# A selective-scan kernel: smaller weight preparation and earlier loads in the head, and one more step between six products and their uses

## The chip, the cores and the metric

The kernel runs on one core of one Trainium2 chip. The time is device time in microseconds (us) from the first to the last instruction. The core has five engines that work at the same time: TensorE (PE, matrix products, with its weight loads PEld shown apart), VectorE (DVE), ScalarE (ACT), GpSimd (POOL) and SyncE (SP), which here only issues DMAs. The kernel before takes 5404.86 us (median of 3 runs, 5400.69 to 5408.01).

## The reference, cut to what matters

The input x is 4 images of 64 x 64 positions with 96 channels. A block of projections with the signs of inputs and weights, a 3 x 3 convolution and a selective scan in four directions is followed by an attention and a feed-forward layer (those last two are in the kernel as "sums", "middle" and "last").

```python
xz = bilinear(x, W_in, s_in, b_in)            # sign(x) @ (s * sign(W - mean)).T + b
xp, z = jnp.split(xz, 2, axis=-1)
t = conv3x3(sign(xc + move0), sc * sign(conv_W)) + conv_b + rp_b0
t = jnp.where(t >= 0, t, prelu_a * t) + rp_b1 + xc
xconv = silu(t)                               # u of the scans, 192 channels
# four orders of the 4096 positions: rows, columns, and both reversed
dts_r, Bs, Cs = split(bilinear(xin, Wl, sl, bl))
delta = softplus(bilinear(dts_r, Wd, sd, bd) + dt_bias)
A = -jnp.exp(A_logs)                          # 192 channels x 16 states, per order

def step(h, inp):                             # 4096 steps per order and image
    ut, dt, Bt, Ct = inp
    h = jnp.exp(dt[..., None] * A[None]) * h + (dt * ut)[..., None] * Bt[:, :, None, :]
    return h, jnp.einsum('bkdn,bkn->bkd', h, Ct)
# ... y of the four orders is added, normed, gated by z; then W_out, residual, attention, feed-forward
```

## The kernel before

The scans are cut into pieces: 4 images x 4 orders (KORD is 1, 3, 0, 2) x 4 stretches of 1024 positions x 6 groups of 32 channels x 4 groups of 4 states, 1536 pieces in all, each a tile of 128 x 1024. Per piece there is a decay dA (ScalarE), an injection (delta u times B), a scan (VectorE), a product with C (on VectorE or GpSimd, whichever has less to do by a running account) and a reduction (TensorE).

```python
def decay(self, i):                    # ScalarE, into one of 2 PSUM tiles
    t = c.p.dA.tile([128, CH], F32, name=f"dA_{i}", tag="dA")
    c.nc.scalar.activation(t, self.dlt[i // NQ][0], AF.Exp, scale=c.anm[:, g, ...])

def inject(self, i):                   # GpSimd
    t = c.p.w.tile([128, CH], F32, name=f"w_{i}", tag="w")
    c.gps.tensor_tensor(t, self.dlt[i // NQ][1], self.bt[b, e, ci, q], ALU.mult)

def run(self, back):                   # Scans
    for _ in self.start(): pass
    self.decay(0)
    for i in range(AHEAD): self.inject(i)          # AHEAD is 3
    for i in range(n):
        self.loads(i)
        if i % NQ == 1:
            while KORD[self.pieces[i][1]] == 2 and self.pieces[i][0] not in c.turned:
                next(back)             # order 2 needs the turned y of orders 1 and 3
            self.load_sums(i)
        ... # carry, decay(i + 1), evacuate, reduce(i - 4), inject(i + AHEAD), product, scan(i)
        next(back, None)               # one step of the background work per piece
```

The background work is a generator that ends a step at each yield: the preparation (prologue) of a later image, the turn of y, and the epilogue of an earlier image.

```python
def back():
    yield from first                   # rest of the prologue of image 0
    yield from prologue(c, 1)
    for b in range(NB):
        while not scans.done(b, 2): yield
        if b not in c.turned: yield from turn(c, b)
        if b + 2 < NB: yield from prologue(c, b + 2)
        e = ends[b]; e.open()
        yield from e.sums(e.lane)      # 8 chunks of 512 positions: norms, W_out, attention sums
        if b + 1 < NB:
            if scans.done(b + 1, 2, 20):
                while not scans.done(b + 1, 2): yield
                yield from turn(c, b + 1)
            yield from e.middle()
            yield from e.last(e.lane)  # 8 chunks: attention output and feed-forward

def turn(c, b):                        # columns to rows, 16 tiles; two halves share one buffer
    ts = [load(*part) for part in parts[:5]]
    yield; yield
    for n, (h, q) in enumerate(parts):
        if q == 0:
            yh = tn.tile([96, L], F32, name=f"yh{h}_{b}", tag="yh")
            for _ in range(4 * h): yield
        yield
        nc.scalar.copy(yh[...], ts.pop(0)[...])
        if n + 5 < len(parts): ts.append(load(*parts[n + 5]))
        if q == NQ8 - 1: nc.sync.dma_start(c.y13[b][h], yh)

# one chunk of the epilogue's norm, cut: each product is used one step later
mm(ps, [(c.mean[:, 0], ys[h]), (c.mean[:, 1], ys[1 - h])])   # yc
yield
nc.scalar.activation(t, sq[h], AF.Square)
mm(ps, [(c.on192, sq[0]), (c.on192, sq[1])])                 # var
yield
nc.scalar.activation(sd, var, AF.Ln, bias=eps)
# ... xc -> xq, xv -> xr, kv -> kvs in the same way; in last(): fv -> fr
```

The head runs before the scans. Two generators take turns: weights() makes the small constants, and the prologue of image 0 ("alone", with the engines to itself) makes the inputs of the scans.

```python
def weights():
    wrow = temp("wrow", [96, 2, 96], F32)          # ln_w broadcast to 96 rows, by DMA
    for rows, h, s in halves(a["pv"][:, :, LN_W]):
        nc.sync.dma_start(wrow[:, h, rows], s.partition_broadcast(96))
    # ... signs of W_in, of the convolution weights, of Wl ...
    # Wd: signs put into zeroed tiles by 8 + 32 copies, 64 transposes, 8 evacuations
    for s in range(8):
        nc.gpsimd.tensor_copy(e[:, :, s, NR * s : NR * s + NR], wds[0])
    for k in range(NK):
        transposed(wdz[0:48, k]..., [e[:, k, s, :] for s in range(8)])
    # ... the same for wdy ...
    for g in range(NG):                            # A, 4 bytes at a time
        src = a["al"][...].rearrange("d k (q j) -> j d (k q)", j=4)
        for j in range(4):
            nc.sync.dma_start(anm[j::4, g, :], src[j])

# prologue of image 0, cut
for q in range(NQ8):                               # x transposed, 8 x 512 columns
    ...; xfin(q, ps)                               # sign by ScalarE, x + b_out by VectorE
nc.gpsimd.memset(xgw[64:128, 1], 0.0)              # clear the padded inputs
for h in range(2): nc.gpsimd.memset(tflat[h].bitcast(F32), 0.0)
# project(h, q): ix, iz products, then signs tp and sz
# convolution in 16 parts: v, r, cz, sign sg (to xg by DMA), e, u; u stored to ud and, turned, to utd
# rows: xg turned (xr), Wl products (acc); B and C (tbc) to bcd, signs (sgn) to sgd, in two halves gh
for x, k in enumerate((o, o + 2)):
    nc.sync.dma_start(gw[:, x, 16:64], c.sgd[b][k]...)
    if fast and x: c.loads_ahead()                 # loads of B and u for the first scans

# Scans.start(), cut
self.next_part = self.prepare(); next(self.next_part)
lanes = [part(0), part(1)]                         # the first deltas, from gT and wdz
while lanes: interleave(lanes)
nc.scalar.activation(c.anm, c.anm, AF.Exp)
nc.vector.tensor_scalar(c.anm, c.anm, -1.0, None, ALU.mult)
for n in range(3):
    ... # two broadcasts of delta and delta u (dl_s), 512 KB each
    if n == 0:
        for q in range(NQ): self.load_bc(1, self.ct, 0, 0, 0, q)     # C
```

Of the kernel before, what the change touches and what calls it, by code (L numbers as in the profile page):

```python
# [53 lines left out]
def hybrid_kernel(ctx: ExitStack, tc: tile.TileContext, a: dict, out: bass.AP):  # L54
# [108 lines left out]
    def weights():  # L163
# [73 lines left out]
        wrow = temp("wrow", [96, 2, 96], F32)  # L237
        for rows, h, s in halves(a["pv"][:, :, LN_W]):
            nc.sync.dma_start(wrow[:, h, rows], s.partition_broadcast(96))
        for rows, h, s in halves(a["pv"][:, :, LN_B]):  # L240
            nc.sync.dma_start(meanw[96:97, 0, h, rows], s.unsqueeze(0))
# [19 lines left out]
        for t in gTs + [wdz]:  # L261
            nc.gpsimd.memset(t.bitcast(F32), 0.0)
# [16 lines left out]
        def scales():  # L279
            part = temp("part", [96, 2, 2])  # L280
            for i in range(2):
                for h in range(2):
                    nc.vector.tensor_reduce(part[:, h, i : i + 1], cwn[h][i], AX.X, ALU.add, apply_absolute_value=True)
            nc.vector.tensor_tensor(csc, part[:, :, 0], part[:, :, 1], ALU.add)
            nc.vector.tensor_scalar(csc, csc, 1.0 / (9 * DN), None, ALU.mult)

            nc.vector.tensor_tensor(cbias, pv[:, :, CONV_B], pv[:, :, RP0], ALU.add)
            nc.vector.tensor_tensor(acs, pv[:, :, PRELU], csc, ALU.mult)
            nc.vector.tensor_tensor(acb, pv[:, :, PRELU], cbias, ALU.mult)
            nc.vector.tensor_tensor(acb, acb, pv[:, :, B_X], ALU.add)  # L290
            nc.vector.tensor_tensor(acb, acb, pv[:, :, RP1], ALU.add)
            nc.vector.tensor_scalar(oma, pv[:, :, PRELU], -1.0, 1.0, ALU.mult, ALU.add)
            for h in range(2):
                nc.gpsimd.tensor_scalar(omad[:, h], i96, oma[:, h : h + 1], None, ALU.mult)
# [5 lines left out]
        for o in range(2):  # L300
# [16 lines left out]
            yield  # L317
            transposed(wR[:, o].rearrange("p x m -> p (x m)"), [we[:, x, :] for x in range(4)])
            yield
            if o == 0:  # L320
                scales()
                yield


        wds = []
        for x, t in enumerate(wd):
            wdm = negmean(f"wdm{x}", t, NR)
            wds.append(temp(f"wds{x}", [128, NK, NR], BF16))
            for k in range(NK):
                nc.scalar.activation(wds[x][:, k, :], t[:, k, :], AF.Sign, bias=wdm[:, k : k + 1])  # L330
        e = temp("wde", [128, NK, 8, 48], BF16)
        nc.gpsimd.memset(e, 0.0)
        for s in range(8):
            nc.gpsimd.tensor_copy(e[:, :, s, NR * s : NR * s + NR], wds[0])
        yield
        for k in range(NK):
            transposed(wdz[0:48, k].rearrange("p s d -> p (s d)"), [e[:, k, s, :] for s in range(8)])
            yield
        for k2 in range(0, NK, 2):
            e = temp(f"wdf{k2}", [128, 2, 8, 128], BF16)  # L340
            nc.gpsimd.memset(e, 0.0)
            for r0 in (0, 64):
                for s in range(8):
                    at = r0 + NR * s
                    nc.gpsimd.tensor_copy(e[r0 : r0 + 64, :, s, at : at + NR], wds[1][r0 : r0 + 64, k2 : k2 + 2])
            yield
            for k in range(2):
                transposed(wdy[:, k2 + k].rearrange("p s d -> p (s d)"), [e[:, k, s, :] for s in range(8)])
                yield
# [11 lines left out]
        nc.vector.memset(mean[:, 1], -1.0 / DN)  # L361
        for h in range(2):
            for o in range(2):
                nc.vector.tensor_tensor(meanw[0:96, h, o], mean[:, int(h != o)], wrow[:, o], ALU.mult)
# [24 lines left out]
        for k in range(NK):  # L389
            o, r0 = k % 2, 64 * (k // 2)  # L390
            nc.sync.dma_start(sbR[r0 : r0 + 32, o, 0:1], a["sl_bc"][0:32, k : k + 1])
            nc.sync.dma_start(sbR[r0 : r0 + 32, o, 1:2], a["bl_bc"][:, 32 * k : 32 * k + 32].rearrange("o p -> p o"))
            nc.sync.dma_start(sbR[r0 + 32 : r0 + 32 + NR, o, :], a["sl_dt"][k])
        for g in range(NG):
            src = a["al"][32 * (g % 4) : 32 * (g % 4) + 32, g // 4].rearrange("d k (q j) -> j d (k q)", j=4)
            for j in range(4):
                nc.sync.dma_start(anm[j::4, g, :], src[j])
# [66 lines left out]
def run(c):  # L464

    scans = Scans(c)
    c.loads_ahead = scans.first_loads
# [63 lines left out]
def prologue(c, b, xts=None):  # L531
# [11 lines left out]
    with tc.tile_pool(name=f"xg_{b}", bufs=1) as xgp:  # L543
# [3 lines left out]
        with tc.tile_pool(name=f"cv_{b}", bufs=1) as cvp:  # L547
# [5 lines left out]


# [35 lines left out]
            def xfin(q, ps):  # L590
                cols = slice(512 * q, 512 * q + 512)
                nc.scalar.activation(xsT[:, cols], ps, AF.Sign, bias=negm, saturate=False)
                t = f32(f"xb{q}")[0:96]
                if alone:
                    nc.vector.tensor_scalar(t, ps, c.bo, None, ALU.add)
                else:
                    nc.scalar.activation(t, ps, AF.Identity, bias=c.bo)
                c.later.store(c.xbd[b][:, cols], t)

            for q in range(NQ8):  # L600
                ps = bank(f"xps{q}", q % 2)[0:96]
                for i in range(4):
                    nc.tensor.transpose(ps[:, 128 * i : 128 * i + 128], xts[q // 2][:, 4 * (q % 2) + i, :], ident)
                yield
                xfin(q, ps)
# [4 lines left out]
            nc.gpsimd.memset(xgw[64:128, 1], 0.0)  # L610
            for h in range(2):
                nc.gpsimd.memset(tflat[h].bitcast(F32), 0.0)
# [99 lines left out]
            def alone_parts():  # L712

                mid = end = None
                for n, part in enumerate(parts + [None, None]):
# [4 lines left out]
                    for s in range(4):  # L720
# [25 lines left out]
                        elif s == 3 and end:  # L746
                            eh, eq, epz, e, en = end
                            u = f32("u" + en)[0:96]
                            c.vec.tensor_tensor(u, epz, e, ALU.mult)
                            c.later.store(c.ud[b][eh][:, 512 * eq : 512 * eq + 512], u)  # L750
# [78 lines left out]
        with tc.tile_pool(name=f"rw_{b}", bufs=1) as rw:  # L829
            xrs = rw.tile([128, 96, 64], BF16, name=f"xr_{b}", tag="xr")  # L830

            tbc = rw.tile([128, L // 2], F32, name=f"tbc_{b}", tag="tbc")
            sgw = rw.tile([128, L // 8], F32, name=f"sgn_{b}", tag="sgn")
            sgn = sgw.bitcast(F8)
            tbg, sgg = (t.rearrange("p (g r) -> p g r", r=64) for t in (tbc, sgn))
# [8 lines left out]
            for o in (1, 0):  # L844
# [30 lines left out]
                for gh in range(2):  # L875
                    groups = slice(32 * gh, 32 * gh + 32)
                    prev = None
                    for n in range(5):
                        if prev is not None:
# [3 lines left out]
                            if fast:  # L883
                                nc.vector.tensor_scalar(tbg[:, :, dv], sv, sc[0], sc[1], ALU.mult, ALU.add)
                            else:
                                nc.scalar.activation(tbg[:, :, dv], sv, AF.Identity, scale=sc[0], bias=sc[1])
# [27 lines left out]
                    for kk in range(2):  # L914
                        k, r0 = o + 2 * kk, 64 * kk
                        nc.sync.dma_start(c.bcd[b][k][:, L // 2 * gh : L // 2 * gh + L // 2], tbc[r0 : r0 + 32, :])
# [3 lines left out]
                        )  # L920
                    yield
# [66 lines left out]
class Epilogue:  # L988
# [143 lines left out]

    def norm(self, ln, q, got):
# [28 lines left out]
        yield  # L1162
        for h in range(2):
# [8 lines left out]
        yield  # L1172
        sd, var, eps = (f32("sd"), ps[0:96], c.eps5[0:96]) if alone else (y0[96:97], ps[96:97], c.eps5[96:97])
# [45 lines left out]
        yield  # L1219
        t = f32("xq")  # L1220
# [3 lines left out]
        yield  # L1224
        r = self.rstd(ln, f"xr{q}", ps)
# [564 lines left out]
```

## Time and profile before

| | value |
|---|---|
| time, median of 3 | 5404.86 us |
| span of the profiled execution | 5405.6 us, 62146 instructions |
| VectorE busy | 5013.4 us (93%) |
| GpSimd busy | 4962.1 us (92%) |
| ScalarE busy | 3617.6 us (67%) |
| TensorE busy | 3405.6 us (63%) |
| GpSimd product, 128 x 1024 | 2359 ns |
| VectorE product, 128 x 1024 | 1225 ns |
| VectorE scan, 128 x 1024 | about 2.3 us |

In a timeline line the columns are start, duration, engine, line, operation, tiles, count, and in brackets the idle time before with what ended it. "SPq" is SyncE's sequencer issuing a DMA[...]. A line of the waits gives the waiting engine with tile and line, the releaser, then total us, times and the longest. Line 435 is a helper that issues VectorE's and GpSimd's operations, so these are told apart by their tiles.

### The profile page before, as it was taken

The page shows a single profiled execution, that of the slowest core. Times are in us where ns is not written, and L with a number is a line of the kernel's source. Part 1 is how long each engine was busy: PE and PEld are TensorE (multiplying, and loading weights), DVE is VectorE, ACT ScalarE, POOL GpSimd, SP SyncE. Part 2 cuts the span into 40 slices and gives each one's busy share as a digit, 9 for nine tenths or more (in the row PEclk, how much of TensorE's full clock was granted, in tenths as well). Part 3 has the DMA queues.
Part 4 walks back from the last instruction along what each step waited for, and adds up shares of the span by engine and source line. Part 5 has one row for each costly group of instructions (what it writes and reads, how often), then busy time and mean ns, then how long its engine had stood idle before and what let it go on. Part 6 is the DMA issues. An engine that isn't in the chain of part 4 may idle for free. (4 is left out here: it accounts for less than half of the span.)

```text
span 5405.6 us, 62146 instructions
## 1 busy us (share of the span) xinstructions
PE 3405.6 (63%) x20083; PEld 1351.6 (25%) x20083; DVE 5013.4 (93%) x3171; ACT 3617.6 (67%) x5648; POOL 4962.1 (92%) x2293
## 2 busy tenths in 40 slices
PE   6456765467755776656775477566776664444577
PEld 3222222122222322222222233122332221111223
DVE  4599999999999999998999999999999999999995
ACT  5567776677766667777777666677656775565554
POOL 3599999999999999999999999999999999999990
PEclk7667876678866787767887688667787666666788
DMA  4665666777766656666765666766665665666652
GB/s 76 158 216 192 192 207 206 227 225 220 218 180 192 220 189 204 217 219 214 225 205 185 199 218 193 245 211 200 207 214 179 192 201 199 189 224 196 214 176 64
DMA packets 635740, 1068.80 MB, mean 198 GB/s; under 512 B 249723, under 2 KB 366740, under 8 KB 633620
## 3 DMA queue, kind: packets, MB, share of 16 engines
q1 hardware_dynamic: 633028, 1063.89, 63.7%
q8 instruction: 157, 2.57, 0.2%
q14 instruction: 171, 1.40, 0.1%
q0 software_dynamic: 1536, 0.79, 0.1%
q10 hardware_dynamic: 848, 0.15, 0.0%
HBM read 829.75 MB, written 228.30 MB: 196 GB/s over the span
## 5 line engine op out<-in xcount | busy, mean ns | idle before, releaser
L435 POOL TENSOR_TENSOR w<-dl,bc 128x1024 f32<-128x1024 f32 x1524 | 3552.0, 2359 | 52.8 <-PE yp L1578 34.8
L1505 ACT ACTIVATE dA<-dl,anm 128x1024 f32<-128x1024 f32 x1524 | 1701.3, 1116 | 490.5 <-DVE w L435 302.2
L435 DVE TENSOR_TENSOR_SCAN dA<-dA,cy,w 128x1024 f32<-128x1024 f32 x725 | 1698.5, 2343 | 75.0 <-ACT dA L1505 60.8
L435 POOL TENSOR_TENSOR w<-h,bc 128x1024 f32<-128x1024 f32 x570 | 1342.9, 2356 | 118.0 <-DVE h L435 111.0
L1578 PE MATMUL yp<-w,sum 128*32 128x256 f32 x12288 | 1249.9, 503 | 294.0 <-ACT pd L1459 204.7
L435 DVE TENSOR_TENSOR w<-dA,bc 128x1024 f32<-128x1024 f32 x966 | 1183.2, 1225 | 69.9 <-DMA bc<-bcd 8.1
L435 DVE TENSOR_TENSOR_SCAN h<-dA,cy,w 128x1024 f32<-128x1024 f32 x427 | 999.1, 2340 | 9.6 <-ACT dA L1505 9.3
L1578 PEld LDWEIGHTS yp<-w,sum 128*32 128x32 f32 x12288 | 316.3, 127 | 1340.5 <-issue 728.3
L1547 ACT COPY cy<-dA 128x1 f32<-128x1 f32 x725 | 114.0, 157 | 757.0 <-DVE w L435 754.7
L435 DVE TENSOR_TENSOR_SCAN dA<-dA,w 128x1024 f32<-128x1024 f32 x241 | 550.0, 2282 | 26.7 <-ACT dA L1505 25.3
L1440 PE MATMUL dps<-gT,wdz 128*128 128x64 fp8e5 x1008 | 113.0, 310 | 375.6 <-ACT ys L1592 373.5
L435 DVE TENSOR_TENSOR_SCAN h<-dA,w 128x1024 f32<-128x1024 f32 x143 | 325.9, 2279 | 24.6 <-POOL w L435 20.5
L1453 PE MATMUL dps<-sp,ident 128*128 128x512 f32 x378 | 269.5, 801 | 101.5 <-ACT dps L1449 101.5
L1583 PE MATMUL yp<-ya,back 128*128 128x256 f32 x576 | 223.4, 506 | 0.0
L1440 PEld LDWEIGHTS <-wdz 128*128 128x128 fp8e5 x1008 | 92.9, 150 | 449.8 <-issue 448.0
L1440 PE MATMUL dps<-gT,wdy 128*128 128x64 fp8e5 x504 | 57.6, 314 | 213.0 <-ACT ys L1592 212.9
L780 PE MATMUL cv<-tp,cwA 128*96 128x512 fp8e5 x432 | 155.2, 478 | 39.1 <-ACT r L812 38.3
L1105 PE MATMUL yc<-eys,mean 96*96 96x512 f32 x240 | 140.1, 738 | 45.6 <-DVE vks L435 23.9
L1547 ACT COPY cy<-h 128x1 f32<-128x1 f32 x427 | 79.2, 186 | 133.5 <-DVE h L435 132.8
L1445 ACT ACTIVATE pd<-dps,dbias,pvd 128x512 f32<-128x512 f32 x189 | 144.0, 762 | 9.8 <-PE dps L1440 9.5
L1583 PEld LDWEIGHTS yp<-ya,back 128*128 128x128 f32 x576 | 116.8, 234 | 119.0 <-issue 90.4
L1446 ACT ACTIVATE sp<-dps,dbias,pvd 128x512 f32<-128x512 f32 x189 | 144.9, 767 | 0.0
(376 smaller groups left out, 4523.6 us busy)
## 6 DMA issues: line engine op xcount, KB each, us to landing
dl<-dld SPq DMA_DIRECT2D x762, 512.0 KB
bc<-bcd SPq DMA_DIRECT2D x512, 512.0 KB
dld<-pd SPq DMA_DIRECT2D x126, 512.0 KB
yd<-ys SPq DMA_DIRECT2D x764, 64.0 KB
dld<-pd SPq DMA_DIRECT2D x126, 256.0 KB
ya<-yd SPq DMA_DIRECT2D x192, 128.0 KB
pu<-ud SPq DMA_DIRECT2D x32, 512.0 KB
pu<-utd SPq DMA_DIRECT2D x31, 512.0 KB
```

What stands on the lines that cost most here:

```text
L435: return getattr(self.eng, name)(out, *args, **kw)
L780: nc.tensor.matmul(ps, w[:, 96 * h : 96 * h + 96], tp[:, 8 * q + dy : 8 * q + dy + 8, dx : dx + IW], start=(w is taps[0][1]), stop=(w is t ...
L1105: self.c.nc.tensor.matmul(ps, w, x, start=(i == 0), stop=(i == len(pairs) - 1))
L1440: nc.tensor.matmul(pv[:, s], wd[:, k, s], gT[:, :, c0 : c0 + 16], start=(s == 0), stop=(s == 7))
L1445: nc.scalar.activation(d[:, 0], ps, AF.Abs, scale=sc, bias=bi)
L1446: nc.scalar.activation(t, ps, AF.Relu, scale=sc, bias=bi)
L1453: nc.tensor.matmul(ps, c.ident, t, start=False, stop=True, skip_group_check=True)
L1505: c.nc.scalar.activation(t, self.dlt[i // NQ][0], AF.Exp, scale=c.anm[:, g, NQ * KORD[e] + q : NQ * KORD[e] + q + 1])
L1547: self.c.nc.scalar.copy(self.carries[g, q], h[:, CH - 1 : CH])
L1578: c.nc.tensor.matmul(y[32 * x : 32 * x + 32, g % 2, :], c.sum4, prod[:, 256 * x : 256 * x + 256], start=(q == 0), stop=(q == NQ - 1 and no ...
L1583: c.nc.tensor.matmul(y[:, g % 2, :], w, src, start=False, stop=(n == len(more) - 1))
```

## The change

The head: the memsets of the padded inputs come first; x is transposed in four pieces of 1024 columns; ln_w and ln_b are broadcast by one product instead of DMAs of single elements; Wd is transposed in two small products and put in place by 24 small DMAs; A comes in one load, its exponential is taken before it is spread, and six DMAs spread it; two parts of u share one store. The second half of B, C and the signs in the first row stage has buffers of its own. u for the first scans is loaded after the first half of that stage, and C together with B ahead of the first deltas. The first injection is VectorE's. In the epilogues of images 0 to 2 a function room() adds one step after each of six products, so that TensorE has longer to finish before ScalarE uses them.

```diff
-        wrow = temp("wrow", [96, 2, 96], F32)
-        for rows, h, s in halves(a["pv"][:, :, LN_W]):
-            nc.sync.dma_start(wrow[:, h, rows], s.partition_broadcast(96))
-        for rows, h, s in halves(a["pv"][:, :, LN_B]):
-            nc.sync.dma_start(meanw[96:97, 0, h, rows], s.unsqueeze(0))
...
-        e = temp("wde", [128, NK, 8, 48], BF16)
-        nc.gpsimd.memset(e, 0.0)
-        for s in range(8):
-            nc.gpsimd.tensor_copy(e[:, :, s, NR * s : NR * s + NR], wds[0])
-        for k in range(NK):
-            transposed(wdz[0:48, k].rearrange("p s d -> p (s d)"), [e[:, k, s, :] for s in range(8)])
...
+            transposed(wdt[x].bitcast(F8), [wds[:, k, :] for k in range(NK)])
...
+            nc.sync.dma_start(wdz.bitcast(F32)[NR * s : NR * s + NR, :, s, :], one)
...
+                nc.sync.dma_start(wdy.bitcast(F32)[at : at + NR, :, s, r0 // 4 : r0 // 4 + 16], two[:, :, 0:16])
...
+        nc.sync.dma_start(al, a["al"].rearrange("p h k s -> p h (k s)"))
+        nc.scalar.activation(al, al, AF.Exp)
+        nc.vector.tensor_scalar(al2, al.rearrange("p h (s j) -> p h j s", j=4), -1.0, None, ALU.mult)
         for g in range(NG):
-            src = a["al"][32 * (g % 4) : 32 * (g % 4) + 32, g // 4].rearrange("d k (q j) -> j d (k q)", j=4)
-            for j in range(4):
-                nc.sync.dma_start(anm[j::4, g, :], src[j])
+            nc.sync.dma_start(anm[:, g, :], al2[32 * (g % 4) : 32 * (g % 4) + 32, g // 4])
...
+            if alone:
+                clear()
...
-            for q in range(NQ8):
+            for q in range(4 if alone else NQ8):
+                if alone:
+                    ps = c.p.dA.tile([128, CH], F32, name=f"xps{q}_{b}", tag="dA")[0:96]
...
+                            if eh:
+                                dst = c.ud[b].rearrange("h p l -> p h l")[:, :, 512 * eq : 512 * eq + 512]
+                                c.later.store(dst, us.rearrange("p (h l) -> p h l", h=2))
...
+                    if fast and gh:
+                        tbcs = [c.p.w.tile([128, CH], F32, name=f"tbc{x}_{b}", tag="w") for x in range(2)]
+                        sgw = c.p.y.tile([128, L // 8], F32, name=f"sgn1_{b}", tag="ys")
...
+                    if fast and gh == 0:
+                        c.first_u()
...
+    def room(self):
+        if self.b < NB - 1:
+            yield
...
         yield
+        yield from self.room()        # after yc, var, xc, xv and kv in norm(), after fv in last()
...
-        c.gps.tensor_tensor(t, self.dlt[i // NQ][1], self.bt[b, e, ci, q], ALU.mult)
+        (c.gps if i else c.vec).tensor_tensor(t, self.dlt[i // NQ][1], self.bt[b, e, ci, q], ALU.mult)
...
+    def first_loads(self):
+        for w, to in enumerate((self.bt, self.ct)):
+            for q in range(NQ):
+                self.load_bc(w, to, 0, 0, 0, q)
...
         lanes = [part(0), part(1)]
+        interleave(lanes)
+        self.next_part = self.prepare()
+        next(self.next_part)
         while lanes:
             interleave(lanes)
-        nc.scalar.activation(c.anm, c.anm, AF.Exp)
-        nc.vector.tensor_scalar(c.anm, c.anm, -1.0, None, ALU.mult)
...
-            if n == 0:
-                for q in range(NQ):
-                    self.load_bc(1, self.ct, 0, 0, 0, q)
```

## The prediction

> **What bounds the kernel now.** I read the page first (part 1 for shares, part 2 for where they hold), then the busy times by window, then the timeline of the first 240 us, then the waits of ScalarE and VectorE in the scan stages.
>
> ```profile
> PE 3405.6 (63%) x20083; PEld 1351.6 (25%) x20083; DVE 5013.4 (93%) x3171; ACT 3617.6 (67%) x5648; POOL 4962.1 (92%) x2293
> ...
> DVE  4599999999999999998999999999999999999995
> ...
> POOL 3599999999999999999999999999999999999990
> ```
>
> VectorE and GpSimd are both full from the second slice on. Only the ends of the digit rows are low: the head, where weights and batch 0 are prepared, and the tail. The windows say it in numbers:
>
> ```profile
> 0.00:250.00 250.00, 135.45 (x759) 73.86 (x759) 114.75 (x176) 129.40 (x216) 101.23 (x171) 0.72 0.60 116
> ...
> 3826.80:4162.90 336.10, 251.65 (x1262) 103.84 (x1262) 312.74 (x203) 206.16 (x329) 315.23 (x138) 0.79 0.65 202
> 4162.90:4488.90 326.00, 216.49 (x1174) 76.15 (x1174) 315.46 (x187) 237.92 (x383) 317.91 (x140) 0.66 0.60 195
> 4488.90:4769.10 280.20, 122.98 (x885) 46.77 (x887) 274.91 (x158) 160.56 (x234) 272.66 (x118) 0.63 0.65 211
> ```
>
> (Columns: PE, weight loads, VectorE, ScalarE, GpSimd, clock, DMA share, GB/s.) Of the first 250 us VectorE works 115. In the scans it works 93% beside the sums of batch 2 (first of the three last rows), 97% beside its last layer, 98% with nothing beside it. So time can come from two places: the start of the scans, and a few per cent of idle VectorE beside the epilogues. The head on the timeline:
>
> ```profile
> 40.59 1.96 POOL L612 MEMSET tp<- 128x1089 f32 x2
> 41.63 0.78 ACT L631 ACTIVATE tp<-ix,sbx,pvx 128x512 fp8e5<-128x512 f32 x1 [4.42 <-POOL tp L612]
> 113.23 17.02 SPq L397 DMA_DIRECT2D anm<-in_al  x24
> 133.50 0.81 DVE L757 TENSOR_SCALAR v<-cv,acs,acb 96x512 f32<-96x512 f32 x1 [9.98 <-DMA ud<-u]
> 167.18 5.75 SPq L770 DMA_DIRECT2D utd<-ut  x2
> 182.00 2.96 DVE L884 TENSOR_SCALAR tbc<-acc,sbR 128x512 f32<-128x512 f32 x4 [5.69 <-DMA bcd<-tbc]
> 187.86 1.53 SPq L927 DMA_DIRECT2D g<-sgd  x2
> 204.14 7.90 SPq L1471 DMA_DIRECT2D bc<-bcd  x4
> 212.36 9.26 POOL L435 TENSOR_TENSOR w<-dl_s,bc 128x1024 f32<-128x1024 f32 x4 [44.12 <-DMA dl_s<-w_s]
> 228.29 2.29 DVE L435 TENSOR_TENSOR_SCAN h<-dA,w 128x1024 f32<-128x1024 f32 x1 [8.37 <-POOL w L435]
> ```
>
> The first convolution input waits for a memset until 41.6 although its product ran at 30.9; the 24 loads of A hold the SyncE queue for 17 us, so stores of u come late and their buffers stop VectorE for 10 us; the scan stage opens at 212.4. In the sums of batch 2:
>
> ```profile
> ACT sq L1165 <- PE yc L1105: 24.4, 12, 2.9
> ...
> ACT kvs L1238 <- PE kv L1233: 8.6, 11, 1.2
> ...
> ACT xq L1221 <- PE xc L1105: 6.9, 5, 2.0
> ACT xr L1110 <- PE xv L1105: 5.9, 5, 2.0
> ACT eys L1174 <- PE var L1105: 5.0, 6, 1.0
> ```
>
> These are the products that get a step more; ScalarE stands still for them, and the decays dA that VectorE needs stand behind them in its queue.
>
> **What the Trainium skill says.** (1) "DMA: Bandwidth & Descriptors", Rules for kernel authors: a strided last dimension becomes one descriptor per element. The trace agrees: the 24 loads of A carry 2 KB each and cost 17.02 us of issue. (2) Same page, Queues, rings and completion order: on each DMA engine a ring's descriptors are consumed in order. Agrees: the loads of C, issued at 204.1, took 7.9 us to issue, and the pair issued just ahead of them was not used before 212.4. (3) "PSUM — Partial Sum Buffer", Engine vs sequencer instructions: the queues of ScalarE, VectorE and GpSimd are strict FIFO. Agrees with the waits above, and it matters for the forced steps below. (4) "GPSIMD Engine Reference", 3.1: an f32 tensor_tensor takes GpSimd 1.96 times VectorE's time; here 2359 against 1225 ns, 1.93 times.
>
> **The change, part by part.**
>
> *Up to the first projection.* The clears (0.96 + 1.96 us) move to the front of GpSimd's queue, where it is idle. The transposes of x go in four pieces of 1024 instead of eight of 512: before they ran from 15.3 to 31.8 us, in a ping-pong of ScalarE (0.68 each) and VectorE (0.74 each). With two larger buffers I count 4 x 2.5 us after the sign of the weights ends at 17.9, so 27. The first tp activation then falls at about 27.5 instead of 41.6. Four projections (two activations of 0.77 each, or three) take 9 us as before, and the first convolution starts near 36.5 instead of 48.5: **12 us**.
>
> *Convolutions.* The 16 parts are seen by the starts of v: 59.2, 66.3, 76.4, 86.8, 94.0, 100.6, 104.8, 108.7, 113.7, 119.1, 133.5, 141.0, 147.5, 151.8, 155.6, 159.3. Undisturbed parts take 4.6 us (100.6 to 119.1; ScalarE works 20.61 of the 22 us from 101 to 123, so that is ScalarE's floor) and 3.9 at the end. The first five intervals (41.4 us) are slow because eight evacuations of 1.22 us on VectorE, memsets and copies of up to 2.3 us on GpSimd and 64 transposes lie between them; these go, and two small evacuations and 24 small DMAs take their place. Three intervals (28.3 us) are slow from the 17 us queue of A, and that becomes one load and six copies. I set the new parts at 7 x 5.8 + 4 x 4.7 + 4 x 3.9 = 75 us against 100.1: 25 saved. With the 12 that makes 37; DMA may take some back, because the eight utd stores (6144 pieces of 64 bytes each) still need 5 to 6 us each. Convolutions end at about **130 instead of 167, 37 us** earlier.
>
> *From there to the scans.* Second-half buffers for B, C and the signs remove 5.7 us on VectorE. But the u loads now stand ahead of the second half's stores in SyncE's order, and they need the last utd stores landed, about 14 us after the convolutions; 0.77 MB of u and 0.5 MB of stores then go ahead of the g load. I expect g some 22 to 23 us after the convolutions, against 187.9 - 167.2 = 20.7: 2 lost. Then eight loads of B and C lie ahead of the first deltas instead of four. At 217 GB/s and a DMA share of 0.84 (190 to 215 us) a full queue moves 258 GB/s, 2 us for 512 KB: 16 us for the eight, 2 for a load of u, 8 for the pair of deltas (issued at 202.8 and used at 212.4, so under 10), with 1.5 us after g: 27.5 us after g, against 212.4 - 187.9 = 24.5. That the deltas no longer wait 2.25 us for u is hidden by this queue: 3 lost. Against that, the second pair of deltas isn't behind C any more, and the first injection costs VectorE 1.2 us instead of GpSimd 2.4; I let the stop of 8.37 us shrink by 3. Sum 2 + 3 - 3 = **2 us lost**. Head: 37 - 2 = **35 us** won.
>
> *Six extra steps.* Counting scans puts the sums of batches 0, 1, 2 at pieces 458-548, 873-963 and 1092-1188. VectorE's idle there is 10.9, 13.2 and 23.4 us; beside the last layer it is 0.105 per piece, so 29 us would be the idle without the waits: 18 to win at most. The work spreads over 130 pieces per batch instead of 90 to 96, out of stretches where idle is only 0.055 per piece, which costs about 6. Net **12 won**.
>
> *The forced turn.* The program walks one background step per piece, so five more steps per chunk cost 40 pieces per batch. Following the steps through, the sums of batch 1 end at piece 1051, not 963. But piece 1057 is the first that needs the turned y of batch 2. The loop there forces the rest of the turn at once: 17 steps, 14 copies of 1.07 us on ScalarE in a row, with the 1.5 MB store of the first half between (the second half uses the same buffer). That is 6.4 us of copies, about 10 us for the store, 8.6 us of copies: 25 us in which no decay is made, against some 6 us of decays in hand. **20 lost**.
>
> Sum: 5404.9 - 35 - 12 + 20 = **5377.9; I say 5377**.
>
> **Rivals.**
> - *The 64-byte stores become the bound of the head.* For: DMA share 0.85 from 142 to 167 us. Eight utd stores at 5.7 us plus u, sz and x come to about 67 us of transfers in a stretch of 90. If they bind, the convolutions end at 140 or later and 10 us of the gain go: 5387. Against: 0.42 between 101 and 123, when parts took 4.6 us.
> - *The forced turn hardly stops VectorE.* For: 5 tiles are already loaded, and the store may be quicker than I think. Then 5 to 10 us are lost, not 20: 5365. Against: in the calm turn the next copy came 14 us after the store's issue, though there four steps set it.
> - *The steps remove the decays' delay altogether,* also in POOL's waits for h (109 us in all): 20 to 30 us won: 5360. Against: beside the last layer, which already waits little for PE, VectorE isn't better than 97%.
> - *Nothing of the head reaches the end,* because another chain sets it. Against: from 212 us on both balanced engines are full, and their work changes by one product only. It would give 5412.
>
> **Range and chances.** Head +-10, steps +-8, forced turn +-8, independent: about +-15, widened for what I haven't seen: 5355 to 5397. Two per cent is 108 us; the whole head before the first scan is 215 us and none of my parts exceeds 40, so within 2% is near certain.
>
> **What would show it.** Right: first tp activation near 28, last utd stores issued near 130, first scan near 180; no evacuations of wdz; ScalarE waits for yc, xc, xv, kv nearly gone; around 3.7 ms a block of 14 yh copies in a row with VectorE idle some 20 us after it begins. Wrong: parts still 6 us apart with stores as releaser (first rival), no idle VectorE at that block (second), VectorE over 97% in the sums (third), or the first scan early and the end unchanged (fourth).

## The result and the profile after

The changed kernel takes 5356.7 us (median of 4 runs, 5351.8 to 5367.6) against 5404.5 us: a ratio of 0.9914 (95% interval 0.9897 to 0.9932), 46.5 us won. Below, "won" and "lost" in us are a ratio's distance from 1 times 5404.5, so that runs measured at different times can be set side by side.

The page of the changed kernel, busy times and slices:

```profile
PE 3387.5 (63%) x20029; PEld 1351.6 (25%) x20029; DVE 5004.4 (93%) x3168; ACT 3606.7 (67%) x5644; POOL 4951.9 (92%) x2254
...
DVE  4699999999999999999999999997999999999995
...
POOL 4699999999999999999999999998999999999990
```

The busy times are almost those of before: the change takes little work away. The second slice is fuller (6 for 5), the 8 near 2.5 ms is gone, and there is a new 7 in the slice from 3615 to 3749 us: the forced turn. By window (columns as in the prediction: PE, weight loads, VectorE, ScalarE, GpSimd, clock, DMA share, GB/s):

```profile
0.00:250.00 250.00, 141.57 (x877) 77.07 (x878) 143.40 (x194) 153.64 (x254) 129.50 (x148) 0.76 0.60 136
3652.30:3695.30 43.00, 12.64 (x67) 4.35 (x66) 18.90 (x13) 23.00 (x32) 20.77 (x10) 0.54 0.72 218
4023.10:4446.40 423.30, 278.56 (x1553) 110.34 (x1550) 418.21 (x264) 263.06 (x425) 418.81 (x184) 0.77 0.63 205
```

VectorE works 143.4 of the first 250 us instead of 114.8. The last row is the sums of batch 2, now 130 pieces long: VectorE is idle for 5.1 of 423.3 us, 1.2% where it had been 7%. The row above is the forced turn, six pieces in 43.0 us, of which VectorE works 18.9. The head on the timeline of the changed kernel (start, duration, engine, line, operation, idle before; L443 is the helper that was line 435):

```profile
25.27 0.77 ACT L653 ACTIVATE tp<-ix,sbx,pvx 128x512 fp8e5<-128x512 f32 x1
36.78 0.81 DVE L783 TENSOR_SCALAR v<-cv,acs,acb 96x512 f32<-96x512 f32 x1 [0.23 <-PE cv L745]
91.48 0.35 SPq L400 DMA_DIRECT2D slab<-in_al  x1
93.28 0.31 ACT L402 ACTIVATE slab<-slab 128x128 f32<-128x128 f32 x1 [7.14 <-DMA slab<-in_al]
93.63 0.27 DVE L403 TENSOR_SCALAR slab<-slab 128x128 f32<-128x128 f32 x1 [9.98 <-ACT slab L402]
135.79 6.25 SPq L796 DMA_DIRECT2D utd<-ut  x2
155.79 1.03 SPq L965 DMA_DIRECT2D g<-sgd  x2
178.84 1.23 DVE L443 TENSOR_TENSOR w<-dl_s,bc 128x1024 f32<-128x1024 f32 x1 [8.59 <-DMA dl_s<-w_s]
191.50 2.29 DVE L443 TENSOR_TENSOR_SCAN h<-dA,w 128x1024 f32<-128x1024 f32 x1 [6.28 <-POOL w L443]
```

The first input of the convolution is there at 25.3 (41.6 before), the last stores of turned u go out at 135.8 (167.2), the first injection runs at 178.8 (212.4), and the scan that stopped for 8.37 us stops for 6.28. But there is a new stop in the middle of the convolutions: A's one load is issued only at 91.48, ScalarE waits 7.14 us for it in order to take its exponential, and VectorE stands 9.98 us behind that. ScalarE's waits in the sums of batch 2 (us in total, times, longest):

```profile
ACT cy L1597 <- DVE w L443: 90.1, 54, 2.8
...
ACT sq L1209 <- PE yc L1143: 4.4, 3, 2.5
ACT eys L1219 <- PE var L1143: 0.3, 1, 0.3
```

Of the waits that the extra steps were to remove, yc went from 24.4 to 4.4 us and var from 5.0 to 0.3; xc, xv and kv don't appear any more. ScalarE now waits for VectorE, so it is ahead. And the forced turn on ScalarE (with SyncE's store of the first half), then on VectorE:

```profile
3648.91 1.12 ACT L1554 ACTIVATE dA<-dl,anm 128x1024 f32<-128x1024 f32 x1 [0.43 <-DVE w L443]
3649.97 3.06 ACT L1015 COPY yh<-yt 96x512 f32<-96x512 f32 x3
3653.89 1.08 ACT L1015 COPY yh<-yt 96x512 f32<-96x512 f32 x1 [0.87 <-DMA yt<-yd]
3659.38 2.03 ACT L1015 COPY yh<-yt 96x512 f32<-96x512 f32 x2 [4.40 <-DMA yt<-yd]
3661.44 0.30 SPq L1022 DMA_DIRECT2D y<-yh  x1
3670.24 7.72 ACT L1015 COPY yh<-yt 96x512 f32<-96x512 f32 x8 [8.83 <-DMA yt<-yd]
...
3677.90 1.14 ACT L1554 ACTIVATE dA<-dl,anm 128x1024 f32<-128x1024 f32 x1
...
3679.14 2.30 DVE L443 TENSOR_TENSOR_SCAN dA<-dA,w 128x1024 f32<-128x1024 f32 x1 [23.96 <-ACT dA L1554]
```

No decay is made from 3650.0 to 3677.9. Half of that time ScalarE isn't copying. It waits 5.3 us for loads of what it is to copy (0.87 and 4.40), and then 8.83 us ahead of the first copy of the second half. The line puts this wait down to a load as well, but that load had landed at 3660.8. The copy also waits for the store of the first half, whose buffer it writes; that store was issued at 3661.44 and landed at 3670.17, and the copy starts at 3670.24. VectorE had 5 us of decays in hand and then stood still for 23.96 us.

### The profile page after: what moved, and what is told of

Read it like the earlier page. It is cut to its first block, busy times and chain, and to the rows that moved or that the text cites. A ratio compares the mean times of both kernels' runs of the same rounds, so it can differ in the third digit from the quotient of the medians.

```text
span 5355.2 us, 61897 instructions
## 1 busy us (share of the span) xinstructions
PE 3387.5 (63%) x20029; PEld 1351.6 (25%) x20029; DVE 5004.4 (93%) x3168; ACT 3606.7 (67%) x5644; POOL 4951.9 (92%) x2254
## 5 line engine op out<-in xcount | busy, mean ns | idle before, releaser
L443 POOL TENSOR_TENSOR w<-dl,bc 128x1024 f32<-128x1024 f32 x1524 | 3549.5, 2355 | 60.3 <-PE yp L1628 43.7
L443 DVE TENSOR_TENSOR_SCAN dA<-dA,cy,w 128x1024 f32<-128x1024 f32 x726 | 1700.7, 2343 | 61.3 <-ACT dA L1554 50.1
L443 POOL TENSOR_TENSOR w<-h,bc 128x1024 f32<-128x1024 f32 x570 | 1341.4, 2353 | 100.5 <-DVE h L443 95.5
L1628 PE MATMUL yp<-w,sum 128*32 128x256 f32 x12288 | 1230.4, 500 | 157.4 <-ACT pd L1508 109.4
L443 DVE TENSOR_TENSOR w<-dA,bc 128x1024 f32<-128x1024 f32 x966 | 1183.3, 1225 | 63.8 <-DMA bc<-bcd 1.9
L443 DVE TENSOR_TENSOR_SCAN h<-dA,cy,w 128x1024 f32<-128x1024 f32 x426 | 996.8, 2340 | 3.4 <-ACT dA L1554 3.1
L443 DVE TENSOR_TENSOR_SCAN dA<-dA,w 128x1024 f32<-128x1024 f32 x240 | 547.7, 2282 | 50.8 <-ACT dA L1554 48.2
L443 DVE TENSOR_TENSOR_SCAN h<-dA,w 128x1024 f32<-128x1024 f32 x144 | 328.1, 2279 | 9.0 <-POOL w L443 8.6
L1280 PE MATMUL kv<-wkv,tt 97*128 97x192 f32 x240 | 76.8, 491 | 136.9 <-DVE tt L443 136.9
L1494 ACT ACTIVATE pd<-dps,dbias,pvd 128x512 f32<-128x512 f32 x189 | 144.0, 762 | 20.9 <-PE dps L1489 20.6
```

The costliest lines, as they stand in the source:

```text
L443: return getattr(self.eng, name)(out, *args, **kw)
L1280: nc.tensor.matmul(pk[i // 2][:, i % 2], tt[:, 128 * i : 128 * i + 128], c.wkv, start=True, stop=True)
L1494: nc.scalar.activation(d[:, 0], ps, AF.Abs, scale=sc, bias=bi)
L1628: c.nc.tensor.matmul(y[32 * x : 32 * x + 32, g % 2, :], c.sum4, prod[:, 256 * x : 256 * x + 256], start=(q == 0), stop=(q == NQ - 1 and no ...
```

## Experiments

Theory after the result: the head gave about 35 us, the extra steps far more than the 12 of the prediction, and the forced turn took about what was predicted. Rivals: the head gave more than it shows at the first scan; or the forced turn cost little and the steps gave 12.

**The parts of the sum.** First the changed kernel without the extra steps, then the kernel before with the extra steps and nothing else.

```diff
     def room(self):
-        if self.b < NB - 1:
-            yield
+        yield from ()
```

> The changed kernel without the extra steps: the epilogues walk as before, and no turn is forced; the head stays changed. Theory now (the steps gave 38 us, the forced turn took 24, net 14): 5357 + 14 = 5371, and the forward idle of VectorE beside the sums is back at 0.12 to 0.24 us per piece. The prediction as written (steps 12, forced turn 20): 5357 - 8 = 5349. Rival: neither matters: 5357.

Measured: ratio 0.9934 (0.9921 to 0.9946), 35.7 us won.

```diff
+    def room(self):
+        if self.b < NB - 1:
+            yield
         yield
+        yield from self.room()        # after yc, var, xc, xv, kv, fv, as in the change
```

> The kernel before with the extra steps alone; everything of the head is as before, and the forced turn at piece 1057 is there. Theory (steps 38, turn 24): 5404.5 - 14 = 5391. The prediction as written (12 against 20): 5412. If the head had changed what the steps are worth (a different balance of products), it would be neither, and this run and the one without steps would not sum to the whole.

Measured: ratio 0.9976 (0.9965 to 0.9986), 13.0 us won, with the forced turn in it: its trace has 63.4 us for the pieces 1051 to 1064. Head 35.7 and steps 13.0 sum to 48.7 against 46.5 for the whole, so the two don't depend on each other, as far as the intervals tell. The prediction had -35 and +8: the head was right, and the pair of steps and turn was wrong in sign.

**The forced turn.** Two ways around it. The first gives the background 25 more steps before it, so that the turn is done in time:

```diff
             next(back, None)
+            if 720 <= i < 920 and i % 8 == 0:
+                next(back, None)
```

> The changed kernel with 25 more background steps, one at each eighth piece from 720 to 919, so that the turn of batch 2 is done before piece 1057 asks for it. Theory (the forced turn stops VectorE for 24 us, and this comes to the end in full): 5357 - 23 = 5334. Rival (the stop is made up for elsewhere, since VectorE and GpSimd have work in hand after it, or the hurried prologue costs as much): 5357. The prediction's term of 20 would give 5337.

Measured: ratio 0.9900 (0.9886 to 0.9913), only 7.6 us better than the changed kernel (two intervals of their own, so +-12: it may be nothing). The windows tell why; the pieces 718 to 921 and then 1051 to 1064 of the changed kernel:

```profile
2540.40:3204.20 663.80, 418.13 (x2719) 163.61 (x2717) 640.42 (x376) 487.26 (x758) 643.17 (x282) 0.75 0.64 204
3633.60:3697.50 63.90, 23.52 (x130) 7.83 (x130) 39.61 (x25) 38.59 (x50) 41.42 (x19) 0.57 0.80 252
```

and the same pieces with the 25 steps:

```profile
2537.30:3214.70 677.40, 437.15 (x2744) 174.08 (x2743) 643.51 (x381) 496.52 (x777) 644.28 (x285) 0.75 0.65 202
3647.90:3689.60 41.70, 23.90 (x125) 7.97 (x125) 39.99 (x24) 29.87 (x46) 40.11 (x18) 0.62 0.80 260
```

The stop is gone (63.9 to 41.7 us, with VectorE's work the same 40 us), but the stretch with the doubled steps takes 13.6 us more, 10.5 of it idle VectorE (23.4 to 33.9). A second step in one piece puts more work on ScalarE ahead of the next decay, which would explain it (not tested). So the run says nothing against the 20 us at the place; of the 22 us it moved 13.6 to an earlier stretch. The second way adds no step: the turn is put between two chunks of the epilogue, as soon as the scans that it needs are done.

```diff
+    def turn_next(self):
+        n = self.b + 1
+        if n < NB and n not in self.c.turned and self.scans.done(n, 2):
+            self.c.later.flush()
+            yield from turn(self.c, n)
# and at the head of each chunk, in sums() and last():
+            yield from self.turn_next()
# and the old place, in back(), does it only if it isn't done
```

> The changed kernel with the turn of the next image's y put between two chunks of the epilogue as soon as its orders 1 and 3 are scanned, with no more steps in all: nothing is forced, and no stretch is hurried. The run with 25 hurried steps took the 22 us out of the six pieces but lost 14 us in the pieces 718 to 921, where those steps were put. Theory (the loss was the hurry, the stop itself comes to the end in full): 22 us under the changed kernel, ratio to the kernel before 0.987 (0.9914 less 0.0041). Rival (VectorE and GpSimd make up for the stop later): as the hurried run, 0.990.

Measured: ratio 0.9886 (0.9873 to 0.9900). That is 15 us better than the changed kernel (two intervals of their own, so +-12), between the two expectations. The turn of batch 2 now runs at pieces 975 to 994, which is where the kernel before has it (975 to 993). Here too the stop is gone: pieces 1051 to 1064 take 43.3 us, 20.6 less, and nothing before them is longer. What comes back is later, in the sums of batch 2:

```profile
4057.30:4493.00 435.70, 297.88 (x1571) 116.06 (x1570) 419.56 (x265) 265.37 (x426) 420.48 (x184) 0.75 0.60 194
```

130 pieces of the same work take 435.7 us, not 423.3: VectorE is idle 16.1 us instead of 5.1. The waits of that stretch, for all engines:

```profile
PE dps L1498 <- ACT ys L1651: 45.7, 8, 6.6
PE op L1143 <- ACT gs L1260: 39.3, 8, 6.3
...
DVE pd L443 <- PE dps L1511: 7.5, 4, 3.1
```

and those of the same sums in the changed kernel:

```profile
PE kv L1280 <- DVE tt L443: 64.0, 8, 9.2
...
PE dps L1489 <- ACT ys L1642: 5.6, 8, 2.0
...
DVE pd L443 <- PE dps L1502: 0.5, 1, 0.5
```

The counts are the point: 8 times, once in each of the 8 chunks, the same product waits for the same thing. With five extra steps a chunk is 16 steps long, one per piece, and the scans start a preparation of deltas every 8 pieces. So each step of the epilogue meets the same stage of that preparation in every chunk, and the piece at which the sums happen to start could decide for all eight whether it is a good meeting. In the changed kernel the sums of batch 2 start at piece 1164, with the turn in the middle at 1181; 8 or 16 pieces later would be the same meeting, 17 is another. The two runs with the hurried steps (the second is under "Both repairs" below) give other starts, 898 for the sums of batch 1 and 1156 for those of batch 2; here the one without the early load of A:

```profile
3140.00:3574.70 434.70, 298.50 (x1594) 114.03 (x1593) 420.13 (x265) 261.87 (x423) 419.89 (x184) 0.79 0.64 202
3991.70:4416.10 424.40, 279.64 (x1544) 110.90 (x1543) 416.68 (x264) 262.11 (x423) 419.98 (x184) 0.76 0.61 198
```

Within batch 2 this fits: 3.26 us per piece from 1156 and 3.26 from 1164, 8 pieces apart, against 3.35 from 1181 (in all three runs with the turn in the middle). Between the batches it doesn't: 898 is 55 times 8 pieces behind 458, where the first sums start, but takes 3.34 us per piece and not 3.24; and with the same start at 921 the runs with the steps take 3.30 to 3.34. So the starting piece alone doesn't set the time, and why the sums from 1181 are slower is not shown.

**The steps alone.** The kernel before, with the steps and with the turn in the middle (both edits are shown above).

> The kernel before with the extra steps and with the turn between two chunks, so that the steps are measured with no forced turn; the head is as before. The prediction's term: 12 won, 5405 - 12, ratio 0.998. Theory (steps are worth 35, as the kernel with steps and forced turn won 13 and the stop in it was 22): ratio 0.9935.

Measured: ratio 0.9950 (0.9938 to 0.9963): 27 us won (20 to 33), 14 more than with the forced turn. The turns of batches 2 and 3 run beside the same pieces as in the kernel before (from 975 and 1358), so the 27 is put down to the steps. The first sums stage, in the kernel before (90 pieces):

```profile
1730.70:2035.00 304.30, 235.94 (x1206) 93.07 (x1210) 293.42 (x193) 197.63 (x314) 293.59 (x129) 0.80 0.62 201
```

and in this kernel (130 pieces):

```profile
1733.50:2155.10 421.60, 290.28 (x1581) 115.56 (x1574) 416.76 (x264) 259.59 (x400) 417.06 (x182) 0.77 0.63 202
```

VectorE's idle time falls from 10.9 to 4.8 us although the stage has 40 pieces more: 0.121 to 0.037 us per piece. So 12 is refuted. 27 is below the 35 expected; as in the run before, the sums of batch 2 start at piece 1181, and they have 16.8 us of idle VectorE, against 5.3 in the run with the steps and the forced turn.

**A's load.** In the changed kernel, the one load of A is moved to the first weights.

```diff
+        al = temp("al", [128, 2, NK * NS])
+        nc.sync.dma_start(al, a["al"].rearrange("p h k s -> p h (k s)"))
         wl = [temp(f"wl{o}", [128, DN], F32) for o in range(2)]
...
-        nc.sync.dma_start(al, a["al"].rearrange("p h k s -> p h (k s)"))
-        yield
```

> The changed kernel with the load of A issued among the first weights. In the changed kernel ScalarE stops 7.1 us for that load and VectorE 10.0 us behind it, and the interval between two convolution parts is 13.7 us there. Theory (that stop is on the path of the head): -8 to -10, 5348, and the last utd stores issued near 127 instead of 135.8. Rival (the utd stores bind the head, so the parts after it wait longer): 5357, last stores still at 135.

Measured: ratio 0.9898 (0.9884 to 0.9911), 8.6 us better than the changed kernel. The same two operations on its timeline:

```profile
82.84 0.29 ACT L402 ACTIVATE slab<-slab 128x128 f32<-128x128 f32 x1
83.16 0.27 DVE L403 TENSOR_SCALAR slab<-slab 128x128 f32<-128x128 f32 x1 [0.51 <-ACT slab L402]
84.59 0.81 DVE L783 TENSOR_SCALAR v<-cv,acs,acb 96x512 f32<-96x512 f32 x1 [0.56 <-PE cv L745]
```

No idle time ahead of the exponential; 4.5 us between two parts where it had been 13.7. The last stores of turned u are issued at 130.4 (135.8) and the scan of piece 4 starts at 192.1 (198.3). One such difference is within the two intervals; the same edit on the two kernels without forced turn below gave 10.8 and 6.5, and there every time with the early load is below every time without it (5341.5 to 5345.0 against 5350.1 to 5357.4, and 5337.6 to 5340.3 against 5342.2 to 5352.7).

The kernel before with A's load as in the change, and nothing else (one load in the place of the 24, exponential first, six DMAs to spread it):

```diff
-                nc.sync.dma_start(anm[j::4, g, :], src[j])             # 24 times
+        nc.sync.dma_start(al, a["al"].rearrange("p h k s -> p h (k s)"))
+        yield
+        nc.scalar.activation(al, al, AF.Exp)
+        nc.vector.tensor_scalar(al2, al.rearrange("p h (s j) -> p h j s", j=4), -1.0, None, ALU.mult)
+            nc.sync.dma_start(anm[:, g, :], al2[...])                  # 6 times
```

> The kernel before with A in one load, its exponential before the spread and six DMAs instead of 24; nothing else. The prediction put three intervals of 28.3 us down to the queue of 17 us, and new parts at 4.7: about 10 to 14 us. Theory: 5404.5 - 10 = 5394. Rival (the 64-byte stores of u alone fill the queue in that stretch): 5402 to 5405.

Measured: ratio 1.0010 (1.0001 to 1.0018), 5 us lost: neither expectation. On the timeline:

```profile
112.92 0.36 SPq L396 DMA_DIRECT2D slab<-in_al  x1
115.13 0.31 ACT L398 ACTIVATE slab<-slab 128x128 f32<-128x128 f32 x1 [10.08 <-DMA slab<-in_al]
115.47 0.27 DVE L399 TENSOR_SCALAR slab<-slab 128x128 f32<-128x128 f32 x1 [12.98 <-ACT slab L398]
```

The 17 us of issue are gone, and a new wait has taken their place. The load stands in SyncE's order behind stores and twelve small loads and goes out at 112.9. In the kernel before no engine waited for A there, since its exponential came only after the first deltas; now an exponential in the middle of ScalarE's queue does. "PSUM — Partial Sum Buffer" of the Trainium skill (Engine vs sequencer instructions) says that this queue is strictly first in, first out, and the trace agrees: everything behind the exponential stood for 10.08 us. The same with the load among the first weights:

> The kernel before with A in one load issued among the first weights, its exponential before the spread, and six DMAs. The run with the same but with the load where the 24 loads stood lost 5 us, with 16.3 us between two convolution parts. Theory (what stops the parts is the place of the load behind the signs' broadcasts, and not how many loads A takes): the intervals of 14 and 16 us shrink to 4 or 5, 8 to 12 us won, ratio 0.998. Rival (the head of before is bound elsewhere): ratio 1.000.

Measured: ratio 0.9983 (0.9977 to 0.9990), 9.2 us won, and the largest interval between two parts is 10.2 us instead of 16.3. One load's place is worth about 15 us (1.0010 against 0.9983), and changes the sign.

**The clears.** The kernel before with only the memsets of the padded inputs moved to the front.

```diff
+            if alone:
+                clear()                    # the three memsets, ahead of the transposes of x
...
-            nc.gpsimd.memset(xgw[64:128, 1], 0.0)
-            for h in range(2):
-                nc.gpsimd.memset(tflat[h].bitcast(F32), 0.0)
+            if not alone:
+                clear()
```

> The kernel before with the clears of the padded inputs moved to the front of GpSimd's queue, nothing else. The first projection input waited for them until 41.6 although its product ran at 30.9. Theory (the first part comes 9 to 10 us earlier, but the weights of the convolution and of A are the next thing waited for): first input near 33, the convolutions end 0 to 5 us earlier, time 5400 to 5405. Rival (every us at the front is a us at the end): 5395.

Measured: ratio 0.9992 (0.9985 to 0.9998), 4 us won. The first input comes at 36.4, not 33:

```profile
29.16 3.92 DVE L283 TENSOR_REDUCE slab<-slab 96x1 f32<-96x960 f32 x4
...
35.80 0.15 DVE L187 TENSOR_SCALAR slab<-slab 128x1 f32<-128x1 f32 x1
...
36.03 0.46 ACT L303 ACTIVATE slab<-slab,slab 128x192 bf16<-128x192 f32 x1 [4.93 <-DMA meanw<-in_pv]
36.39 0.76 ACT L638 ACTIVATE tp<-ix,sbx,pvx 128x512 fp8e5<-128x512 f32 x1
```

ScalarE's next operation, the sign of a weight, waits 4.93 us. The line names a load of ln_b, but the last part of that load landed at 36.26, after the sign had begun. What the sign needs is the mean of its weight, and VectorE finishes that at 35.95 (the operation at 35.80), in order behind four reductions of convolution weights and two evacuations of x. The clears alone give 5.2 of the 16.4 us that the changed kernel has at this place; the next wait was already standing behind them. How the other 11 us divide among the rest of the change was not tested.

**The loads of B, C and u.** The changed kernel with these loads where the kernel before had them.

```diff
-                    if fast and gh == 0:
-                        c.first_u()
...
-        for w, to in enumerate((self.bt, self.ct)):
-            for q in range(NQ):
-                self.load_bc(w, to, 0, 0, 0, q)
+        for q in range(NQ):
+            self.load_bc(0, self.bt, 0, 0, 0, q)
+        self.first_u()
...                                          # C again after the first pair of deltas
```

> The changed kernel with the loads of u, B and C where the kernel before had them (u and B after the second half's first signs, C after the first deltas); the buffers of the second half stay. The prediction: the moved loads cost 2 + 3 us and give back 3, so undoing them gives about -2: 5355. Rival (the loads are what made the first scans come early, since the stop of the second scan fell by 2 us and piece 4 gained 2.2 more): 5360. In the trace the first scan, the stop ahead of scans 2 to 4 and the start of piece 4 tell.

Measured: ratio 0.9914 (0.9901 to 0.9928), the same as the changed kernel. The timeline shows what balances:

```profile
151.18 1.41 SPq L963 DMA_DIRECT2D g<-sgd  x2
...
176.53 1.23 DVE L443 TENSOR_TENSOR w<-dl_s,bc 128x1024 f32<-128x1024 f32 x1 [7.29 <-DMA dl_s<-w_s]
...
193.60 2.29 DVE L443 TENSOR_TENSOR_SCAN h<-dA,w 128x1024 f32<-128x1024 f32 x1 [10.69 <-POOL w L443]
```

Counted from the last stores of u (134.65 here), g is issued 16.5 us later (20.0 with the early loads), the first injection comes 25.4 us after g (23.1), and the later stop is 10.69 us (6.28). At piece 4 the early loads are 3.3 us ahead (62.5 against 65.8 after the stores). At the end that doesn't show within the interval.

**Both repairs.** The hurried steps and the early A, then the turn in the middle and the early A.

> The changed kernel with the 25 spread background steps and with the one load of A issued among the first weights instead of behind the loads of the signs. Theory: -23 for the turn and -8 to -10 for the head: 5325. Rivals: the stores of u bind the head, so the earlier load gives nothing: 5334; both nothing: 5357.

Measured: ratio 0.9880 (0.9867 to 0.9894), 10.8 us better than the hurried steps alone.

> The changed kernel with both: the turn between two chunks, and A loaded among the first weights. Theory: 22 + 9 us under the changed kernel, ratio to the kernel before 0.9857, about 5331 us. Rival (the stop is made up for later): 0.9885.

Measured: ratio 0.9874 (0.9859 to 0.9889), 68 us won against 46.5 of the change, the fastest version here (5338.7 us beside 5409.2 for the kernel before in the same comparison). It lies between the theory and the rival, as the turn in the middle alone did.

## Why the prediction was right, and where it was not

The predicted 5377 is 20 us above what came out: the sum was -27 and is -46.5. The stated range (5355 to 5397) holds the result by less than 2 us, so that it holds is partly luck. The head came out as sized, and so did the forced turn at its place; the term that was mis-sized is the six extra steps, 12 for 27, which is outside the +-8 given for it.

- **Head, 35 won.** Measured 35.7 at the end of the whole, 34.6 at the first scan, 36.8 at piece 4. The sum is right because errors cancel:
  - *First convolution 12 earlier.* It came 17.7 earlier (48.5 to 30.8). The four projections before it were put at "9 us as before" and took 5.6; in the kernel before they take 6.9 (41.63 to 48.50), so the 9 was a misreading. The first input came at 25.3, not 27.5. A further 4.8 us that the prediction did not have: from the first convolution product to the first v are 6.0 us instead of 10.7, so that v starts at 36.8 (59.2).
  - *16 parts in 75 us.* The intervals sum to 91.4 (100.1 before): 8.7 saved, not 25. This term failed. The prediction counted the removed loads, but not that what replaces them brings waits of its own: the one load of A (with A early its interval falls from 13.7 to 4.5, and the last stores come 5.4 sooner), and probably the 24 small DMAs of Wd, whose issues fill SyncE's queue from 55 to 75 us while three intervals are 8 to 10 us; a run without them was not made.
  - *From there to the scans 2 lost.* From the last stores to piece 4 the path shrank from 67.9 to 62.5: 5.4 won. g came 20.0 us after the stores, not 22 to 23, and the deltas were used 23.1 after g, not 27.5. The 16 us for the eight loads of B and C were right: the first is issued at 156.86, and the last has landed at 173.0. What was too long is the end: u landed 1.3 us later (2 predicted), and the pair of deltas at 178.7, 4.4 us after u, where 8 had been put, although the prediction's own 258 GB/s gives 4 us for 1 MB. From the first injection to piece 4 it is 19.5 us instead of 22.8, the 3 us predicted.
- **Six extra steps, 12 won.** Measured 27 (20 to 33). The step that failed is the floor: "beside the last layer it is 0.105 per piece, so 29 us would be the idle without the waits". With the steps the sums idle 0.037 to 0.13 us per piece, and 0.037 in the first of them is a third of that floor. So the idle beside the last layer is no floor for the sums. ScalarE is busier there (0.73 of the time, against 0.62 in the first sums with the steps), which may be why; this was not tested. The third rival (20 to 30 won) had it right, and named the sign: VectorE works 98.9% in the first sums.
- **Forced turn, 20 lost.** At the place it is right: 27.9 us without a decay, 5 in hand, 23.96 idle, 20 to 22 less where it is taken away. Its time is made up as predicted, copies 6.2 (6.4), store 8.8 (10) and copies 7.7 (8.6), with 5.3 us of waits for loads on top, which the prediction had not. At the end, taking it away won 14 and 15 (and 8 with the hurried steps); where it won 14 and 15, the sums of batch 2 then start at another piece and have 11 us more of idle VectorE.
- **Rivals.** The 64-byte stores do not bind the head: with A early, everything after came sooner. The forced turn does stop VectorE. The head does reach the end.

## What to carry to other kernels

Before a load is made smaller or its use moved, look at where it stands in the queue that issues it and at what the first user holds up: the same single load lost 5 us in one place and won 9 in another. Don't take the idle time of a neighbouring stage as the floor of the stage to be mended. When a stop is removed by moving work, measure the stretch that receives it, and those behind it, which then start at another place. Where a wait has several conditions, look when each was met before blaming the one that a line names: twice here a load was named, and a store or VectorE's work ended the wait.

## What the runs showed of the hardware that was not expected

- A small load costs little to carry and much to stand behind: the load of A takes 0.35 us to issue and is used 1.8 us after that (91.48 to 93.28), but its place in the queue cost ScalarE 7.14 us in one kernel and 10.08 in another.
- A turn in a hurry is half waiting: of the 27.9 us, the fourteen copies take 13.9. Waits for their loads take 5.3, with five buffers to load into, and 8.8 go to one store of 1.5 MB (8.7 us from issue to landing) that holds the only output buffer.
